# A gated cross-attention and router block on one core: the third piece of c gets another buffer and an earlier load, and the fillers of the last three pairs change places

## The chip, the core and the metric

The kernel runs on one core of a Trainium2 chip. The core has a matrix engine (TensorE, in the profile PE; its weight loads, which overlap with it, are PEld), a vector engine (VectorE, DVE), a scalar engine (ScalarE, ACT), a general engine (GpSimd, POOL) and a queue engine (SyncE, SP) that issues most of the transfers; ACT issues a few as well. Each engine runs its own instructions in the order in which they are written, and engines wait for each other through semaphores. The metric is the device time of one execution in microseconds, the median of several executions; lower is better.

## What is computed

The inputs are x and c, each 8 batches of 512 rows by 2048 columns in f32. Columns are cut into windows of 128. Cut to its core, the reference is

```python
n = layernorm(x, axis=-1)                      # over the 2048 columns of a row
q, k = Wq @ n + bq, Wk @ n + bk                # 256 rows each, per window
val = Wv @ c + bv
scores = q_h.T @ k_h / sqrt(32)                # 8 heads, 128 x 128 per window
o = gelu(softmax(masked(scores)) @ val_h)      # per head
x = x + tanh(g_xattn) * (Wo @ o + bo) * mask
flat = layernorm(x, axis=-1)                   # again over the 2048 columns
s = softmax(flat @ router_weight.T + router_bias)        # 64 experts
w = s with all but its 8 largest set to 0
x = x + tanh(g_ffn) * (flat * w.sum() + w @ expert_bias)
```

## The kernel before

**Tiling.** 512 columns make a chunk `ch` (0 to 31, four to a batch) and 256 columns, two windows, make a pair `g` (0 to 63), so that pair g is half `h = g % 2` of chunk `g // 2`. The 512 rows of x and c are four groups m of 128 partitions. `cx` tiles hold a half chunk of c (128 x 4 x 256, 512 KB), and two buffers of them rotate; `o` tiles (128 x 2 x 512, of the same size) hold the attention output of a chunk, also in two buffers.

**The start.** SP and ACT issue the loads of the weights, of x of batch 0 in 16 tiles of 256 KB (four groups m, four chunks j) and of the first c pieces (lines 153 to 174). PE first makes the values `pv = c.T Wv` of the pieces (0,0), (0,1) and (1,0) (`values`, L404, its products at L410), and then the first queries and keys (`first_queries_and_keys`, L332, products `pf` at L339), one group m after the other. Group m needs the normalised x of that group: DVE takes its statistics (L263, four of them, and L246), POOL turns them into a scale and a shift in a chain of small instructions (L248 to L276), ACT applies them (`norm`, L284). The piece (1,0) has to wait until PE has read the first buffer of `cx`.

**The loop.** Slots g = 0 to 61 (L789) each run the scores of pair g, the softmax (maxima on DVE at L454, exponentials on ACT at L463, division on POOL at L472), the transposes of pair g-1 (`turn` on PE at L486, its copy on ACT at L492), the weighing of pair g-2 (`weigh`, L505, copy L515), and fillers for PE: queries and keys of the next chunk (L373), its values (L410), the output projection (`attend`, L534), transposes of finished x (`turn_x`, L558), router logits (L572), the choice of experts (`select`, L632, on DVE; `turn_weights`, L655, two transposes `pw` on PE at L661, and a copy on ACT at L665) and the mix of the experts' biases (`mix`, L691, with the addition on DVE at L702). The order on every engine is that in which the lines stand; nothing is rescheduled. The choice of experts for the batch that ended before falls on every eighth slot, the last of these being slot 60.

Each slot has the values of the next chunk among its fillers, by

```python
vals = [] if (nxt, h) == (1, 0) or nxt == last else [(nxt, h)]    # L806
```

so that slots 60 and 61, whose next chunk is the last (31), have none. In slot 60 the part behind the queries and keys runs

```python
turn_x_(2)
for c_, h_ in vals:
    values(c_, h_, 0, 0)
    turn_(2)
    values(c_, h_, 1)
...
turn_weights(b4)
```

**The end.** Pairs 62 and 63 (`h0` and `g`, lines 998 to 1050) are written out by hand. `z` is chunk 31 and `b` is batch 7, so `turn_x(z - 2, k)` transposes columns of chunk 29 and `mix(b - 1, k)` finishes part k of batch 6. Values of (31,0) stand in pair 62, values of (31,1), two mixes and the four transposes of chunk 29 in pair 63. The transposes of attention, `turn_x` and the product of `weigh` share two PSUM buffers (tag `tr`); a buffer comes free when the copy out of it is done, which is ACT's for `turn` and `weigh`, and DVE's for these `turn_x`. Projections, values and mixes share two others (tag `mm`).

Of the kernel before, what the change touches and what calls it, by code (L numbers as in the profile page):

```python
# [9 lines left out]
F32 = mybir.dt.float32  # L10
# [6 lines left out]
P = 128  # L17
# [18 lines left out]
def flamingo_gated_kernel(  # L36
# [23 lines left out]
    nc = tc.nc  # L60
# [6 lines left out]
    NM = D // P  # L67
# [5 lines left out]
    HW = NPP * W  # L73
    NH = CW // HW
# [9 lines left out]
    work = ctx.enter_context(tc.tile_pool(name="work", bufs=2))  # L84
# [6 lines left out]
    def columns(ch):  # L91
        return slice((ch % NCH) * CW, (ch % NCH + 1) * CW)

    def rows_of(t, b, cs):
        return t[b, :, cs].rearrange("(m p) s -> p m s", p=P)
# [13 lines left out]
        nc.sync.dma_start(t, rows_of(x, ch // NCH, columns(ch)))  # L109
        xn[ch] = t  # L110

    def load_cx(ch, h, queue=nc.sync):
        t = work.tile([P, NM, HW], F32, tag="cx", name=f"cx_{ch}_{h}")
        s0 = (ch % NCH) * CW + h * HW
        queue.dma_start(t, rows_of(c, ch // NCH, slice(s0, s0 + HW)))
        cxs[ch, h] = t

    def load_mask(ch):
        t = work.tile([P, CW], F32, tag="mk", name=f"mk_{ch}", bufs=4)
        nc.sync.dma_start(t, masks[ch // NCH, :, columns(ch)].to_broadcast([P, CW]))  # L120
        mks[ch] = t

    def load_xr(ch, queue=nc.sync):

        t = work.tile([P, NM, CW], F32, tag="xr", name=f"xr_{ch}", bufs=6)
        queue.dma_start(t, rows_of(x, ch // NCH, columns(ch)))
        xr[ch] = t
# [20 lines left out]
    def load_first_x(m):  # L148
        for j in range(NCH):
            queue_ = nc.scalar if j >= NCH // 2 and m < NM - 1 else nc.sync  # L150
            queue_.dma_start(xr[j][:, m, :], x[0, m * P : (m + 1) * P, columns(j)])

    nc.sync.dma_start(wv_sb, wvT.rearrange("(m p) e -> p m e", p=P))
    load_cx(0, 0, nc.scalar)
    load_first_x(0)
    load_cx(0, 1)
    nc.sync.dma_start(wq_sb, wqT.rearrange("(m p) e -> p m e", p=P))
    nc.scalar.dma_start(wk_sb, wkT.rearrange("(m p) e -> p m e", p=P))
    load_first_x(1)

    def load_rest():
        load_cx(1, 0)
        load_first_x(2)
        load_first_x(3)
        load_mask(0)
        nc.sync.dma_start(bv_sb, bv.partition_broadcast(P))
        with nc.allow_non_contiguous_dma(reason="short bias vectors onto partitions"):
            nc.sync.dma_start(bq_sb, bq.rearrange("(t p) -> p t", p=P))
            nc.sync.dma_start(bk_sb, bk.rearrange("(t p) -> p t", p=P))
            nc.sync.dma_start(bo_sb, bo.rearrange("(t p) -> p t", p=P))  # L170
        nc.sync.dma_start(gates[:, 0:1], g_xattn.partition_broadcast(P))
        nc.sync.dma_start(gates[:, 1:2], g_ffn.partition_broadcast(P))
        nc.sync.dma_start(rb_sb, rb.partition_broadcast(P))
        load_mask(1)
# [148 lines left out]
    def product(shape, name, r=None):  # L323

        if late:
            late.append(late.pop(0))
            r = late[0]
        if r is not None:
            return ps_sc.tile(shape, F32, tag=f"sc{r}", name=name)
        return ps_mm.tile(shape, F32, tag="mm", name=name)  # L330
# [73 lines left out]
    def values(ch, h, i, r=None):  # L404

        if (ch, h) not in pvs:
            pvs[ch, h] = product([P, NPP, DK], f"pv_{ch}_{h}", r)
        cx, pv = cxs[ch, h], pvs[ch, h]
        for m in range(NM):
            nc.tensor.matmul(  # L410
                pv[:, i, :], cx[:, m, i * W : (i + 1) * W], wv_sb[:, m, :],
                start=(m == 0), stop=(m == NM - 1),
            )

    def values_out(ch, h):
        pv = pvs.pop((ch, h))
        del cxs[ch, h]
        vT = work.tile([P, NPP, DK], F32, tag="vT", name=f"vT_{ch}_{h}", bufs=4)
        nc.vector.tensor_tensor(vT, pv, bv_sb[:, None, :].to_broadcast([P, NPP, DK]), ALU.add)
        vTs[ch, h] = vT  # L420
# [35 lines left out]
    def exps(g, q):  # L456

        p = pairs[g]
        i = q // 2
        for r in (2 * (q % 2), 2 * (q % 2) + 1):  # L460
            for e in range(NE):
                h = e * HR + r
                nc.scalar.activation(  # L463
                    p["at"][i][:, h, :], p["sc"][r][:, i, e, :], AF.Exp,
                    bias=p["nmx"][:, r, i, e : e + 1], accum_out=p["rsum"][:, i, h : h + 1],
                )

    def divide(g, i, engine=None):
        p = pairs[g]
        rs = p["rsum"][:, i, :]  # L470
        nc.vector.reciprocal(rs, rs)  # L471
        (engine or nc.gpsimd).tensor_tensor(  # L472
            p["at"][i], p["at"][i], rs[:, :, None].to_broadcast([P, H, W]), ALU.mult
        )
# [3 lines left out]
    def turn(g, k):  # L478

        p = pairs[g]  # L480
        i, e = k // NE, k % NE
        if e == 0:
            p["atT"][i] = work.tile([P, H, W], F32, tag="atT", name=f"atT_{g}_{i}")
        pt = ps_tr.tile([P, HR, W], F32, tag="tr", name=f"pt_{g}_{k}")
        for r in range(HR):
            nc.tensor.transpose(pt[:, r, :], p["at"][i][:, e * HR + r, :], ident)  # L486
        p["pt"] = pt

    def turned(g, k):
        p = pairs[g]  # L490
        i, e = k // NE, k % NE
        nc.scalar.copy(p["atT"][i][:, e * HR : (e + 1) * HR, :], p.pop("pt"))  # L492
# [33 lines left out]
    def gelu(ch, cs=whole):  # L526
        o = os_[ch][:, :, cs]
        nc.scalar.activation(o, o, AF.Gelu)
# [26 lines left out]
    def turn_x(ch, k, engine=None):  # L555
        px = ps_tr.tile([P, NM, P], F32, tag="tr", name=f"px_{ch}_{k}")
        for m in range(NM):
            nc.tensor.transpose(px[:, m, :], xr[ch][:, m, k * P : (k + 1) * P], ident)  # L558
        t = work.tile([P, NM, P], F32, tag="x1T", name=f"x1T_{ch}_{k}", bufs=4)
        if engine is nc.vector:  # L560
            nc.vector.tensor_copy(t, px)
        else:
            nc.scalar.copy(t, px)  # L563
        x1T[ch, k] = t
# [117 lines left out]
    def mix(b, k, hold=False):  # L682

        t = experts[b]
        j, mp = k // 2, k % 2
        js = slice(j * CW, (j + 1) * CW)
        held[b, k] = []
        for i in range(2):
            rows = slice(i * E, (i + 1) * E)
            pt = product([P, CW], f"pb_{b}_{k}_{i}")  # L690
            nc.tensor.matmul(pt, t["wT"][rows, mp, :], eb_sb[rows, js], start=True, stop=True)  # L691
            held[b, k].append(pt)
        if not hold:
            added(b, k)

    def added(b, k, queues=(nc.sync,)):
        j, mp = k // 2, k % 2
        ch = b * NCH + j
        n = 2 // len(queues)
        for i, pt in enumerate(held.pop((b, k))):  # L700
            xc = xr[ch][:, 2 * mp + i, :]
            nc.vector.tensor_tensor(xc, pt, xc, ALU.add)  # L702
            if (i + 1) % n == 0:
                ms = slice(2 * mp + i + 1 - n, 2 * mp + i + 1)
                queues[i // n].dma_start(rows_of(out, b, columns(ch))[:, ms, :], xr[ch][:, ms, :])
        if mp == 1:
            del xr[ch]
# [26 lines left out]
    for i in range(NPP):  # L734
        values(0, 0, i)
    new_queries_and_keys(0)
    load_rest()

    nc.scalar.activation(spare, half[:, 0:1], AF.Identity)
# [29 lines left out]
    queue = [(b, i) for b in range(1, B) for i in range(NPIECE)]  # L769
# [17 lines left out]
    last = NC - 1  # L787
    pieces_left = [(b, i) for b in range(1, B) for i in range(NPIECE)]
    for g in range(NG - NH):  # L789
        ch, h = g // NH, g % NH  # L790
        even = h == 0
        nxt = ch + 1
# [10 lines left out]
        lch = ch - 2 if not even and ch >= 2 else None  # L803
        pch = ch - 1 if not even and ch >= 1 else None

        vals = [] if (nxt, h) == (1, 0) or nxt == last else [(nxt, h)]  # L806
        b4 = ch // NCH - 1
        fin = g % SPB if b4 >= 0 else None

        def turn_(k):  # L810
            if g1 is not None:
                turn(g1, k)
                turned(g1, k)
# [172 lines left out]
    z, b, h0 = last, B - 1, NG - NH  # L986
# [20 lines left out]
    divide(h0, 0)  # L1007
    turn_(h0 - 1, 0, 1)
    exps(h0, 2)
    values(z, 0, 0)  # L1010
    turn_(h0 - 1, 2)
    exps(h0, 3)
    values(z, 0, 1)
    values_out(z, 0)
    turn_(h0 - 1, 3)
    divide(h0, 1)

    scores(g)
    weigh(h0 - 1)
# [2 lines left out]
    maxima(g, (2, 3))  # L1022
    turn_(h0, 0)
    exps(g, 0)
    mix(b - 1, 2)
    turn_(h0, 1)
    exps(g, 1)
    divide(g, 0)
    values(z, 1, 0)
    turn_x(z - 2, 0, nc.vector)  # L1030
    exps(g, 2)
    values(z, 1, 1)
    values_out(z, 1)
    exps(g, 3)
    divide(g, 1)
    turn_(h0, 2)
    turn_x(z - 2, 1, nc.vector)
    turn_(h0, 3)
    turn_x(z - 2, 2, nc.vector)
    gelu(z - 1)  # L1040
    mix(b - 1, 3)
    load_xr(z)
    turn_x(z - 2, 3, nc.vector)
    weigh(h0)
    weighed(h0)
    for k in (4, 5):
# [110 lines left out]
```

## Time and profile before

| | us |
|---|---|
| median of 3 runs (1336.63 to 1337.97) | 1337.61 |
| the profiled execution | 1337.72 |
| its span, first to last instruction | 1335.9 |
| PE busy | 1306.5 |
| DVE, ACT, POOL busy | 887.2, 836.0, 793.1 |
| mean granted clock of PE, as a share of full speed | 0.995 |
| transfers, 173.32 MB in all | 130 GB/s on average |

The profiled execution is 0.11 us above the median, and its span leaves 1.8 us of it to what lies before the first and behind the last instruction. Times below are microseconds from the start of the span. A row of a timeline gives start, duration, engine, line, operation, the tiles, how often, and in brackets how long the engine had been idle before it and what ended that idle time. A row of waits gives the time in total, how often, and the longest. A row of a stretch gives its length, the busy time and count of each engine in it, PE's granted clock, the share of the DMA engines and GB/s. The page's "chain that ended last" is the path of work, followed back from the last instruction, that set the time.

### The profile page before, as it was taken

What the parts mean: (1) busy time and instruction counts of PE and PEld (TensorE: products, weight loads), DVE (VectorE), ACT (ScalarE), POOL (GpSimd) and SP (SyncE); (2) the same over time, 40 slices, a digit from 0 to 9 for tenths busy, and PEclk for the clock granted to TensorE, in tenths of its full rate; (3) what the DMA queues carried; (4) which work ended last, traced back from release to release, by engine and by line L of the source; (5) the groups of instructions that cost most, each with busy time, mean ns of one, the idle gap of its engine ahead of it and who ended that gap; (6) DMA issues with size and microseconds to landing.
All of it is one profiled execution on the core that took longest, in us unless ns stands there. A gap on an engine that the chain in (4) does not pass through costs nothing.

```text
span 1335.9 us, 26509 instructions
## 1 busy us (share of the span) xinstructions
PE 1306.5 (98%) x9802; PEld 953.6 (71%) x9802; DVE 887.2 (66%) x1815; ACT 836.0 (63%) x2843; POOL 793.1 (59%) x802
## 2 busy tenths in 40 slices
PE   7999999999999999999999999999999999999997
PEld 4677777777777777777777777777777777777653
DVE  5666666576766766677666676667676675666566
ACT  2567756666755666756667566667656767656653
POOL 3545556565566755667555667556566665566652
PEclk8999999999999999999999999999999999999999
DMA  9423332334443534443534443524544423332124
GB/s 290 117 73 124 98 103 99 131 105 133 150 163 115 166 102 136 150 146 131 166 100 138 151 148 130 166 89 135 165 146 132 156 65 120 135 112 87 64 80 173
DMA packets 109729, 173.32 MB, mean 130 GB/s; under 512 B 9248, under 2 KB 43680, under 8 KB 109472
## 3 DMA queue, kind: packets, MB, share of 16 engines
q1 hardware_dynamic: 107536, 168.75, 39.1%
q10 hardware_dynamic: 2064, 2.88, 0.6%
q8 instruction: 77, 1.26, 0.4%
q14 instruction: 52, 0.43, 0.1%
HBM read 138.06 MB, written 33.55 MB: 128 GB/s over the span
## 4 chain that ended last, share of the span: by engine, by line
PE 93%; DVE 3%; ACT 2%; DMA 1%; issue 0%; DVEq 0%; ACTq 0%
PE qk L373 27%; PE po L534 17%; PE pv L410 15%; PE pt L486 8%; PE pa L505 5%; PE pb L691 5%; PE pl L572 4%; PE sc L442 4%; PE px L558 4%; PE sc L433 2%; ACT at L463 1%; PE pf L339 1%; DMA cx<-in_ctx 1%; DVE st L553 1%; DVE st L263 1%; PE pg L602 1%
## 5 line engine op out<-in xcount | busy, mean ns | idle before, releaser
L472 POOL TENSOR_TENSOR at<-at,rsum 128x1024 f32<-128x1024 f32 x128 | 244.3, 1908 | 282.2 <-DVE rsum L471 259.6
L463 ACT ACTIVATE at<-sc,nmx 128x128 f32<-128x128 f32 x1024 | 364.9, 415 | 5.8 <-DVE nmx L454 5.8
L463 ACT ACTIVATION_READ_ACCUMULATOR at<-sc,nmx 128x1 f32 x1024 | 261.4, 255 | 0.0
L410 PE MATMUL pv<-wv_sb,cx 128*128 128x256 f32 x1024 | 242.7, 386 | 9.8 <-DMA cx<-in_ctx 9.6
L534 PE MATMUL po<-o,wo_sb 128*128 128x512 f32 x512 | 234.0, 599 | 0.0
L410 PEld LDWEIGHTS pv<-wv_sb,cx 128*128 128x128 f32 x1024 | 191.4, 194 | 33.8 <-DMA cx<-in_ctx 10.0
L543 POOL TENSOR_TENSOR xr<-t,xr 128x512 f32<-128x512 f32 x124 | 160.4, 1294 | 88.7 <-DVE t L540 88.2
L515 ACT COPY o<-pa 128x512 f32<-128x512 f32 x64 | 37.5, 585 | 258.2 <-PE pa L505 258.2
L492 ACT COPY atT<-pt 128x512 f32<-128x512 f32 x256 | 151.4, 622 | 56.2 <-PE pt L486 55.7
L454 DVE TENSOR_REDUCE nmx<-sc 128x4 f32<-128x512 f32 x256 | 158.7, 682 | 12.0 <-PE sc L442 12.0
L534 PEld LDWEIGHTS po<-o,wo_sb 128*128 128x128 f32 x512 | 94.2, 190 | 100.1 <-issue 92.8
L540 DVE SCALAR_TENSOR_TENSOR t<-po,bo_sb,mk 128x512 f32<-128x512 f32 x128 | 95.9, 750 | 100.6 <-PE po L534 99.9
L486 PEld LDWEIGHTS pt<-ident,at 128*128 128x128 f32 x1024 | 122.0, 141 | 56.9 <-issue 36.4
L486 PE MATMUL pt<-ident,at 128*128 128x128 f32 x1024 | 150.8, 275 | 1.3 <-ACT atT L492 1.1
L563 ACT COPY x1T<-px 128x512 f32<-128x512 f32 x120 | 70.3, 585 | 118.8 <-PE px L558 117.1
L373 PE MATMUL qk<-xt,wq_sb 128*128 128x256 f32 x496 | 128.2, 381 | 1.3 <-DVE u L381 1.3
L373 PE MATMUL qk<-xn,wk_sb 128*128 128x256 f32 x496 | 127.6, 380 | 0.0
L373 PE MATMUL qk<-xn,ws 128*128 128x256 f32 x496 | 127.3, 379 | 0.0
L373 PEld LDWEIGHTS qk<-xn,ws 128*128 128x128 f32 x496 | 94.2, 190 | 12.8
L702 DVE TENSOR_TENSOR xr<-pb,xr 128x512 f32<-128x512 f32 x124 | 79.2, 684 | 33.0 <-PE pb L691 33.0
L373 PEld LDWEIGHTS qk<-xn,wk_sb 128*128 128x128 f32 x496 | 89.3, 190 | 10.0 <-DVE lgT L588 0.3
L678 POOL TENSOR_SCALAR xr<-xr,xa,xd 128x512 f32<-128x512 f32 x120 | 94.4, 797 | 0.8
(119 smaller groups left out, 2008.4 us busy)
## 6 DMA issues: line engine op xcount, KB each, us to landing
cx<-in_ctx SPq DMA_DIRECT2D x63, 512.0 KB, 5.4
out_dram<-xr SPq DMA_DIRECT2D x60, 512.0 KB, 3.5
raw<-in_x SPq DMA_DIRECT2D x112, 256.0 KB, 3.5
xn<-in_x SPq DMA_DIRECT2D x28, 1024.0 KB, 7.5
xr<-in_x SPq DMA_DIRECT2D x28, 1024.0 KB, 7.8
mk<-in_mask_Bx1x_ff SPq DMA_DIRECT2D x32, 256.0 KB, 5.4
xr<-in_x SPq DMA_DIRECT2D x10, 256.0 KB, 5.9
out_dram<-xr SPq DMA_DIRECT2D x7, 256.0 KB, 2.3
```

Source lines behind the costliest of these rows:

```text
L373: nc.tensor.matmul(out_, w_[:, j, es], xb[:, j, :], start=(j == 0), stop=(j == NM // 2 - 1))
L410: nc.tensor.matmul(pv[:, i, :], cx[:, m, i * W : (i + 1) * W], wv_sb[:, m, :], start=(m == 0), stop=(m == NM - 1),)
L454: nc.vector.tensor_reduce(p["nmx"][:, r, :, :], p["sc"][r], AX.X, ALU.max, negate=True)
L463: nc.scalar.activation(p["at"][i][:, h, :], p["sc"][r][:, i, e, :], AF.Exp, bias=p["nmx"][:, r, i, e : e + 1], accum_out=p["rsum"][:, i, h ...
L472: (engine or nc.gpsimd).tensor_tensor(p["at"][i], p["at"][i], rs[:, :, None].to_broadcast([P, H, W]), ALU.mult)
L486: nc.tensor.transpose(pt[:, r, :], p["at"][i][:, e * HR + r, :], ident)
L492: nc.scalar.copy(p["atT"][i][:, e * HR : (e + 1) * HR, :], p.pop("pt"))
L534: nc.tensor.matmul(po[:, cs], wo_sb[:, e, m * P : (m + 1) * P], os_[ch][:, e, cs], start=(e == 0), stop=(e == NE - 1),)
L540: nc.vector.scalar_tensor_tensor(t[:, cs], po[:, cs], bo_sb[:, m : m + 1], mks[ch][:, cs], ALU.add, ALU.mult)
L543: (engine or nc.gpsimd).tensor_tensor(xc, t[:, cs], xc, ALU.add)
L678: nc.gpsimd.tensor_scalar(xc, xc, a, d, ALU.mult, ALU.add)
L702: nc.vector.tensor_tensor(xc, pt, xc, ALU.add)
```

## The change

Three things change. `load_cx` takes a tag, and the piece (1,0) of c is loaded into a buffer of the tag `o`, with its load issued ahead of Wq and of the second group of x. The values of (31,0) move from pair 62 to slot 60. The fillers of pairs 62 and 63 are dealt anew: the second mix, two transposes of chunk 29 and the first half of the values of (31,1) move from pair 63 to pair 62; the fourth mix and the load of x for chunk 31 stand earlier in pair 63.

```diff
-    def load_cx(ch, h, queue=nc.sync):
-        t = work.tile([P, NM, HW], F32, tag="cx", name=f"cx_{ch}_{h}")
+    def load_cx(ch, h, queue=nc.sync, tag="cx"):
+        t = work.tile([P, NM, HW], F32, tag=tag, name=f"cx_{ch}_{h}")
...
     load_cx(0, 1)
+
+    load_cx(1, 0, tag="o")
     nc.sync.dma_start(wq_sb, wqT.rearrange("(m p) e -> p m e", p=P))
     nc.scalar.dma_start(wk_sb, wkT.rearrange("(m p) e -> p m e", p=P))
     load_first_x(1)
 
     def load_rest():
-        load_cx(1, 0)
         load_first_x(2)
...
-        vals = [] if (nxt, h) == (1, 0) or nxt == last else [(nxt, h)]
+        vals = [] if (nxt, h) in ((1, 0), (last, NH - 1)) else [(nxt, h)]
...
     divide(h0, 0)
     turn_(h0 - 1, 0, 1)
     exps(h0, 2)
-    values(z, 0, 0)
+    mix(b - 1, 2)
     turn_(h0 - 1, 2)
     exps(h0, 3)
-    values(z, 0, 1)
-    values_out(z, 0)
     turn_(h0 - 1, 3)
+    turn_x(z - 2, 0, nc.vector)
+    turn_x(z - 2, 1, nc.vector)
     divide(h0, 1)
+    values(z, 1, 0)
 
     scores(g)
...
     turn_(h0, 0)
     exps(g, 0)
-    mix(b - 1, 2)
+    values(z, 1, 1)
+    values_out(z, 1)
     turn_(h0, 1)
     exps(g, 1)
     divide(g, 0)
-    values(z, 1, 0)
-    turn_x(z - 2, 0, nc.vector)
+    turn_x(z - 2, 2, nc.vector)
     exps(g, 2)
-    values(z, 1, 1)
-    values_out(z, 1)
+    mix(b - 1, 3)
+    load_xr(z)
     exps(g, 3)
     divide(g, 1)
     turn_(h0, 2)
-    turn_x(z - 2, 1, nc.vector)
+    turn_x(z - 2, 3, nc.vector)
     turn_(h0, 3)
-    turn_x(z - 2, 2, nc.vector)
     gelu(z - 1)
-    mix(b - 1, 3)
-    load_xr(z)
-    turn_x(z - 2, 3, nc.vector)
     weigh(h0)
```

## The prediction

> **What bounds the kernel now.** First the busy shares and the chain of waits.
>
> ```profile
> PE 1306.5 (98%) x9802; PEld 953.6 (71%) x9802; DVE 887.2 (66%) x1815; ACT 836.0 (63%) x2843; POOL 793.1 (59%) x802
> PE 93%; DVE 3%; ACT 2%; DMA 1%; issue 0%; DVEq 0%; ACTq 0%
> ```
>
> PE is the bound. The change gives PE no less to do, so it can only gain from time in which PE stands still or runs slowly. That is 1335.9 - 1306.5 = 29.4 us of idleness, of which 6.5 lie before the first product and 7.5 behind the last. PE's own waits name the rest that is large:
>
> ```profile
> PE pv L410 <- DMA cx<-in_ctx: 9.6, 2, 6.5
> PE pw L661 <- DVE rest L648: 3.0, 1, 3.0
> ```
>
> The 9.6 are the first wait of 6.5 and one of 3.1. PE's timeline shows where these two idle times lie, and what follows them: the start (four rows), then slot 60 (three rows).
>
> ```profile
> 6.48 9.91 PE L410 MATMUL pv<-wv_sb,cx 128*128 128x256 f32 x32 [6.48 <-DMA cx<-in_ctx]
> 19.48 6.78 PE L410 MATMUL pv<-wv_sb,cx 128*128 128x256 f32 x16 [3.09 <-DMA cx<-in_ctx]
> 26.10 1.88 PE L339 MATMUL pf<-xn,wq_sb 128*128 128x512 f32 x4
> 36.40 1.88 PE L339 MATMUL pf<-xn,wq_sb 128*128 128x512 f32 x4
> ```
> ```profile
> 1232.99 0.60 PE L486 MATMUL pt<-ident,at 128*128 128x128 f32 x4
> 1236.55 0.44 PE L661 MATMUL pw<-ident,rest 128*128 128x128 f32 x2 [2.95 <-DVE rest L648]
> 1238.06 2.08 PE L691 MATMUL pb<-eb_sb,wT 64*128 64x512 f32 x4
> ```
>
> After each, PE is slow: 16 products of values take 6.62 us (19.48 to 26.10), and four mixes 2.08, where they take 1.13 elsewhere. The stretches show why; the number behind POOL's is the granted clock.
>
> ```profile
> 19.40:21.00 1.60, 1.52 (x4) 1.25 (x5) 0.86 (x2) 0.00 (x0) 1.27 (x6) 0.50 1.06 389
> 1233.00:1235.00 2.00, 0.59 (x6) 0.35 (x4) 1.93 (x9) 1.07 (x2) 0.96 (x1) 1.00 0.00 0
> 1238.50:1239.50 1.00, 1.00 (x4) 0.07 (x2) 0.00 (x0) 0.25 (x1) 1.00 (x2) 0.50 0.00 0
> ```
>
> The clock is halved from about 18.9 to 25.6 and from 1237.4 to 1240.9, after the idle time.
>
> **Part 1, the third piece of c.** The load of (1,0) waits until PE has read the first buffer, is issued at 12.97 and lands at 19.44. Changed, it waits for no reader. In the changed program's order it takes the place that Wq's load had on SP, behind the landing of c's piece (0,0): issue at 6.45. Wq in that place landed 8.8 us later (row of its transfer), so the piece lands at about 15.3, before PE ends with (0,1) at 16.39. The 3.09 us go, and with them the halved clock: warm, 16 products take 3.46 (the values of other slots stand in the chain of waits with 3.46). PE is ready for `pf` at 16.39 + 3.46 = 19.85 instead of 26.10, **6.25 earlier**.
>
> Next late is x. In the trace `pf` needs 3.43 per group (26.10, 29.54, 32.97, 36.40) and x is there in time: normalised x of group 1 starts at 21.32, of group 3 at 29.23, each tile 0.8. But SP's queue now carries 512 KB more ahead of group 1, and SP waits longer: x of group 1 was issued at 7.70 behind the landing of an x tile, and is now issued behind (0,1) and Wk, at 12.2 to 12.5. The stretches from 3.2 to 23 run at 355 to 389 GB/s with DMA share above 1, so no reordering makes the whole faster: what had landed by 19.44 (all but six x tiles) is what will have landed when group 1 is complete, so its last tile comes at 18 to 19.4; I take 19.2. From there by the durations of the trace: three more statistics to 21.1; then 2.84 from there to ACT (18.48 to 21.32) and 0.8, so group 1 at 24.75 against PE's 19.85 + 3.43 = 23.28: a wait of 1.45. DVE does group 2 to 24.0 and group 3 to 26.8 (2.56 plus 0.27 each); group 3 needs 3.91 more (25.32 to 29.23) and 0.8: 31.5, against PE's 24.75 + 2 x 3.43 = 31.6. So the last `pf` group starts at 31.6 instead of 36.40: **4.8**. Ends: x at 18.0 leaves 6.1; x another 1.5 us later leaves 3.3. I round the middle to **5.0**. Everything behind (sums of x on POOL, first softmax) hangs on the same chain and moves along. The second buffer rotation costs nothing: (1,1) is needed 30 us after its load, and `o` is first written in slot 2.
>
> **Part 2, slot 60.** The values of (31,0), 3.46, now stand between `pt` and `pw`. Slot 52, where they always stood, shows PE without a wait:
>
> ```profile
> 1074.39 1.89 PE L410 MATMUL pv<-wv_sb,cx 128*128 128x256 f32 x8
> 1076.12 0.38 PE L661 MATMUL pw<-ident,rest 128*128 128x128 f32 x2
> ```
>
> PE reaches `pw` at 1232.99 + 0.43 + 3.46 = 1236.9, DVE's `rest` is there at 1236.5. The wait of 2.95 and the slow clock go. Warm, `pw`, two transposes and the mix take 0.22 + 0.44 + 0.53 + 1.06 = 2.2, so pair 61 begins at 1239.1, and its weighing at 1240.3 instead of 1241.65: **1.35 earlier**, though 3.46 of work came in. The DVE addition of 0.69 for these values follows `select` and delays nothing that PE waits for.
>
> **Part 3, pairs 62 and 63.** Here 3.46 has gone, yet ACT paces the pair. Its copies in the trace:
>
> ```profile
> 1266.11 0.59 ACT L492 COPY atT<-pt 128x512 f32<-128x512 f32 x1
> 1268.22 0.58 ACT L492 COPY atT<-pt 128x512 f32<-128x512 f32 x1
> 1277.60 0.63 ACT L492 COPY atT<-pt 128x512 f32<-128x512 f32 x1
> 1278.98 0.58 ACT L492 COPY atT<-pt 128x512 f32<-128x512 f32 x1 [0.75 <-PE pt L486]
> ```
>
> With the scores of pair 62 left where they were (1257.05), PE now does mix (1.06 from 1263.68) and two transposes, and is through at 1265.65. The next transpose needs the buffer of the third `pt`, whose copy stands on ACT behind four exponentials that end at 1266.0: 1266.5. The one after it needs DVE's copy (0.69): 1267.85. Then 0.43 and 1.73 of values: scores of pair 63 at 1270.0 instead of 1268.11. Pair 63 has lost 3.66 of PE work, but the fourth `pt` waits for the third's copy, which stands behind all eight exponential groups: 10.35 after the scores; its own copy ends at 11.55, and `weigh` ends at 11.9 where it ended at 13.86 (1268.11 to 1281.97). Sum: 12.95 + 11.9 = 24.85 against 11.06 + 13.86 = 24.92. The 3.46 us less work is eaten by new waits; only slot 60's 1.35 remains. At the next meeting point (`pt`, then `attend` of chunk 30 at 1284.77) PE waits about 0.3 for ACT's copy behind GELU. I count **1.2** for parts 2 and 3. The earlier load of x (31) shortens nothing: it landed 2 us before its use. The mix's addition, moved ahead, costs DVE 1.3 in a pair where it is busy for 5.63 of 11.1.
>
> **A rule against it.** PE waits in pair 63 from 6.85 to 8.05 and 8.5 to 10.35 after the scores, with one transpose (0.43) between. The row of slot 60 says that a hole of 2.95 followed by transposes halves the clock for 3.4 us, at a cost of about 1.7. [...] By the row alone (a window with 0.9 of 3.4 busy was enough) the window must fall well: about 3 in 10. [...] Sum by the one 5.0 + 1.2, by the other 5.0 - 0.3. No trace shows a hole filled with one transpose; I lean to the row and keep both ends.
>
> **Cases.** The sum is made against the profiled 1337.72, 0.11 above the median.
> - *Both parts as worked out*, 0.48: 1337.7 - 6.2 = **1331.5**, own range 1330.3 to 1332.5.
> - *Clock halved in pair 62 or 63*, 0.28: 1.5 back, 1333.0 (1332.5 to 1334.5). [...]
> - *x comes later or in worse order*, 0.11: the start gains 2.5, the rest 0.6: 1334.6. For it: the moved issues at 12.2; against: saturated transfers.
> - *ACT is no pace* (copies earlier than I place them, holes filled), 0.08: slot 60's 2.95 + 1.7 and 0.6 of small waits come out whole: 1337.7 - 5.0 - 5.2 = 1327.5. Against: ACT's rows stand back to back from 1263.5 to 1268.7.
> - *Piece (1,0) still late*, so that only the end changes, 0.02: 1336.5.
> - *Slower*, 0.03: SP's loads form a chain, each behind the landing of an earlier one, and with one more large load ahead the last x tiles slip. They land at about 23.5 now; PE has 6.4 in hand on group 3 as it stands. From a landing about 6 + 2.7 later, at 32, PE is later than before by more than can be told apart: 1341. The saturated stretches speak against it.
>
> Range 1329.3 to 1334.8. What a measurement can tell from no change is about 0.2%, 2.7 us, so 1334.9 and below is faster: 0.48 + 0.27 + 0.07 + 0.08 = 0.90; within 0.2% 0.07; slower 0.03.
>
> **What would show it.** `pv` of (1,0) starts without a wait at 16.4 with clock 1.00; a wait of 1 to 2 us before the second `pf` group; scores of pair 0 at about 35 instead of 39.9; `pw` of slot 60 without a wait; new PE waits on ACT's L492 and DVE's copies of about 1.7 us in pair 62 and 3 in pair 63. Wrong if `pf` starts at 19.9 but its last group not before 34, if the clock is 0.50 behind pair 63, or if pairs 62 and 63 run without these waits.

## The result, and the profile after

| | before | after |
|---|---|---|
| median, us | 1337.26 | 1334.11 |
| lowest to highest of 16 runs each | 1333.41 to 1338.19 | 1332.85 to 1335.98 |
| the profiled execution | 1337.72 | 1334.19 |
| its span | 1335.9 | 1332.4 |

The changed kernel is faster: ratio 0.9978, 95% interval 0.9971 to 0.9986. It moved by 3.15 us (3.53 between the two profiled executions), about half of the 6.2 that were forecast. The page after, busy shares and the chain that ended last:

```profile
PE 1303.9 (98%) x9802; PEld 951.6 (71%) x9802; DVE 887.1 (67%) x1815; ACT 837.1 (63%) x2843; POOL 794.3 (60%) x802
PE 92%; DVE 3%; DMA 2%; ACT 1%; issue 1%; POOL 0%; SPq 0%; DVEq 0%; ACTq 0%
```

PE still runs 9802 instructions, and its busy time fell by 2.6 us: a slow clock shows as busy time (the four mixes of slot 60 are 2.08 of it before and 1.13 after), so time won at the clock shows here. PE's waits (total, times, longest):

```profile
PE pv L411 <- DMA cx<-in_ctx: 6.8, 1, 6.8
PE pt L487 <- ACT atT L493: 2.6, 2, 1.8
...
PE px L559 <- DVE x1T L562: 1.6, 2, 0.8
PE pf L340 <- ACT xn L285: 1.4, 1, 1.4
```

The second wait for c (3.1) and the one of `pw` (3.0) are gone. In their place stand the three last rows, of which the prediction had named all: normalised x at `pf`, ACT's copy of a `pt`, DVE's copy of a `px`. Of the 2.6 behind ACT's copies only the 1.8 are new; a wait of 0.8 early in the loop was there before. The start in PE's timeline:

```profile
6.75 13.52 PE L411 MATMUL pv<-wv_sb,cx 128*128 128x256 f32 x48 [6.75 <-DMA cx<-in_ctx]
20.11 1.88 PE L340 MATMUL pf<-xn,wq_sb 128*128 128x512 f32 x4
...
25.11 1.98 PE L340 MATMUL pf<-xn,wq_sb 128*128 128x512 f32 x4 [1.41 <-ACT xn L285]
...
32.08 1.88 PE L340 MATMUL pf<-xn,wq_sb 128*128 128x512 f32 x4
```

All 48 products of values stand in one row without a hole. The one wait behind them is 1.41, and the last `pf` group starts at 32.08 instead of 36.40. Slot 60:

```profile
1231.05 1.89 PE L411 MATMUL pv<-wv_sb,cx 128*128 128x256 f32 x8
1232.78 0.38 PE L662 MATMUL pw<-ident,rest 128*128 128x128 f32 x2
...
1233.96 1.13 PE L692 MATMUL pb<-eb_sb,wT 64*128 64x512 f32 x4
...
1236.24 1.08 PE L506 MATMUL pa<-atT,vT 128*32 128x128 f32 x32
```

`pw` no longer waits, and the four mixes take 1.13 instead of 2.08: the granted clock is 1.00 from 1233.9 to 1235.1, where before it was 0.50 from 1237.9 to 1240.1. The last row is the weighing in slot 61, which before started at 1241.65:

```profile
1241.65 1.08 PE L505 MATMUL pa<-atT,vT 128*32 128x128 f32 x32
```

Now the place where time was lost, pairs 62 and 63:

```profile
1261.17 0.63 PE L559 MATMUL px<-ident,xr 128*128 128x128 f32 x4 [0.60 <-issue]
1262.58 0.66 PE L559 MATMUL px<-ident,xr 128*128 128x128 f32 x4 [0.78 <-DVE x1T L562]
...
1264.90 0.40 PE L434 MATMUL sc<-mneg,negw 32*128 32x512 bf16 x4
...
1272.83 0.66 PE L559 MATMUL px<-ident,xr 128*128 128x128 f32 x4 [0.81 <-DVE x1T L562]
1275.30 0.89 PE L487 MATMUL pt<-ident,at 128*128 128x128 f32 x4 [1.81 <-ACT atT L493]
1276.12 1.94 PE L506 MATMUL pa<-atT,vT 128*32 128x128 f32 x32
1277.99 2.41 PE L573 MATMUL pl<-x1T,rw_sb 128*64 128x512 f32 x8
```

The two holes of pair 63 (0.81 and 1.81) are there with one group of transposes between them, and behind them PE is slow: the weighing takes 1.94, where it takes 1.08 in slot 61. The stretches of the hole and of what follows it (busy time of each engine; the number behind POOL's is the granted clock):

```profile
1272.15:1275.57 3.42, 0.92 (x6) 0.69 (x7) 2.59 (x6) 3.10 (x17) 2.29 (x2) 1.00 0.19 75
1275.57:1279.00 3.43, 3.43 (x40) 2.01 (x40) 0.00 (x1) 2.74 (x3) 3.43 (x4) 0.50 0.50 135
```

PE was busy for 0.92 of 3.42 us, 27%, and the granted clock was then 0.50 for a stretch as long.

### The profile page after: what moved, and what is told of

Its sections match the earlier page's. It is cut to its first block, busy times and chain, and to the rows that moved or that the text cites. A ratio compares the mean times of both kernels' runs of the same rounds, so it can differ in the third digit from the quotient of the medians.

```text
span 1332.4 us, 26505 instructions
## 1 busy us (share of the span) xinstructions
PE 1303.9 (98%) x9802; PEld 951.6 (71%) x9802; DVE 887.1 (67%) x1815; ACT 837.1 (63%) x2843; POOL 794.3 (60%) x802
## 4 chain that ended last, share of the span: by engine, by line
PE 92%; DVE 3%; DMA 2%; ACT 1%; issue 1%; POOL 0%; SPq 0%; DVEq 0%; ACTq 0%
PE qk L374 27%; PE po L535 17%; PE pv L411 15%; PE pt L487 8%; PE pa L506 5%; PE pb L692 5%; PE pl L573 4%; PE sc L443 4%; PE px L559 4%; PE sc L434 2%; ACT at L464 1%; PE pf L340 1%; DVE st L264 1%; DMA cx<-in_ctx 1%; DVE st L554 1%; PE pg L603 1%
## 5 line engine op out<-in xcount | busy, mean ns | idle before, releaser
L411 PE MATMUL pv<-wv_sb,cx 128*128 128x256 f32 x1024 | 239.4, 383 | 6.8 <-DMA cx<-in_ctx 6.8
```

The source lines that it names most:

```text
L411: nc.tensor.matmul(pv[:, i, :], cx[:, m, i * W : (i + 1) * W], wv_sb[:, m, :], start=(m == 0), stop=(m == NM - 1),)
```

## The experiments

Each is compared with the kernel before on the same chip; (n) is the number of runs. Every edit starts from the changed kernel.

### The start alone

The buffer and the earlier load stay; slot 60 and pairs 62 and 63 go back to what they were.

```diff
-        vals = [] if (nxt, h) in ((1, 0), (last, NH - 1)) else [(nxt, h)]
+        vals = [] if (nxt, h) == (1, 0) or nxt == last else [(nxt, h)]
...
```

(The fillers of pairs 62 and 63, as they stood before, are left out here.)

> The start of the change alone (c's third piece early, in a buffer of o), slots 60 to 63 as before. Theory: the start is worth 4.1 us (the scores of pair 60 came 4.1 earlier in the changed trace), x of group 1 is its limit, and slot 60 keeps its wait of 2.95 and its halved clock: 1333.2, as fast as the whole change or faster. Rival, that the two parts share one gain (what the start saves is lost again in a later wait, and the end brings the rest): 1335 or more.

Median 1333.34 (9), against 1336.42 (21): ratio 0.9977, interval 0.9967 to 0.9986. That is as much as the full change gains (0.9978). In its PE timeline slot 60 is as it was, only 4.5 us earlier (`pw` stood at 1236.55):

```profile
1232.06 0.44 PE L662 MATMUL pw<-ident,rest 128*128 128x128 f32 x2 [2.96 <-DVE rest L649]
...
1233.71 2.08 PE L692 MATMUL pb<-eb_sb,wT 64*128 64x512 f32 x4
```

The wait of 2.96 and the slow mixes stand, and pair 63 has no halved clock (1.00 from 1270 to 1280, and its weighing takes 1.08). So what the other two parts win in slot 60 (the change's own trace shows it) is lost again elsewhere.

### The end alone

```diff
-    load_cx(1, 0, tag="o")
...
     def load_rest():
+        load_cx(1, 0)
         load_first_x(2)
```

> The end of the change alone, the start as before. Theory: slot 60 gives 1.3, pairs 62 and 63 take 1.9 back through copies that wait behind ACT's exponentials and a halved clock: 1337.8, within 0.6 of before, and where the clock is not halved behind pair 63, 1336.6. Rival, that the end gains (values in slot 60 are worth their 4.6 us of wait and slow clock): 1333 to 1335.

Median 1336.72 (13), against 1336.42: ratio 0.9999, interval 0.9990 to 1.0007. Slot 60's values and the new deal of pairs 62 and 63 together are worth nothing that can be measured; a gain of more than 1.3 us (0.0010 of 1336.4) lies outside the interval. Its profiled execution had the full clock in pair 63 (1.00 from 1275 to 1280, the weighing 1.17), and there the last row of mixes starts at 1319.21, where before it started at 1319.90: 0.7 us.

### Group 1 of x ahead of Wq

The timeline of SP's queue after the change shows what the new load pushed back: x of group 1 is issued at 12.22 (before: 7.70).

```profile
2.22 4.89 SPq L115 DMA_DIRECT2D cx<-in_ctx  x2
7.66 0.37 SPq L159 DMA_DIRECT2D wq_sb<-in_L_xattn_Wq  x1
12.22 7.70 SPq L151 DMA_DIRECT2D xr<-in_x  x8
```

```diff
     load_cx(1, 0, tag="o")
+    load_first_x(1)
     nc.sync.dma_start(wq_sb, wqT.rearrange("(m p) e -> p m e", p=P))
     nc.scalar.dma_start(wk_sb, wkT.rearrange("(m p) e -> p m e", p=P))
-    load_first_x(1)
```

> The whole change, with the second group of x issued ahead of Wq and Wk. Theory: x of group 1 is what PE waits for (1.41) at the start; with 512 KB less ahead of it on SP it is complete 1.2 us earlier, Wq lands last but in time for 20.1, the wait shrinks to 0.2 and all groups move by about 1.2: 1332.9. Rival, that transfers are saturated and one wait only takes the place of the other (Wq or Wk late): no better than 1334.1, the wait under Wq's or Wk's name.

Median 1332.23 (5), against 1336.42: ratio 0.9963, interval 0.9950 to 0.9977. DVE's timeline, after the change first, then this kernel:

```profile
18.86 2.54 DVE L264 BATCH_NORM_STATS2 st<-xr 128x6 f32<-128x512 f32 x4 [7.66 <-DMA xr<-in_x]
```
```profile
15.81 2.56 DVE L264 BATCH_NORM_STATS2 st<-xr 128x6 f32<-128x512 f32 x4 [4.72 <-DMA xr<-in_x]
```

Group 1's statistics start 3.05 earlier, and PE's wait for x is gone: in this kernel's PE timeline no `pf` shows a wait, and the last group starts at 29.98 instead of 32.08.

```profile
19.45 1.96 PE L340 MATMUL pf<-xn,wq_sb 128*128 128x512 f32 x4
...
22.96 1.88 PE L340 MATMUL pf<-xn,wq_sb 128*128 128x512 f32 x4
...
26.40 1.88 PE L340 MATMUL pf<-xn,wq_sb 128*128 128x512 f32 x4
...
29.98 1.98 PE L340 MATMUL pf<-xn,wq_sb 128*128 128x512 f32 x4
```

So after the change x of group 1 is what the start waits for, and the order of the loads sets it. The first product came earlier in this profile too (6.08, not 6.75), but that is not the reason: in the run with DVE copies below it came at 6.20, with Wq ahead of x, and the last `pf` group still started at 31.89.

### Copies of the last `pt` on DVE

The third and fourth copies of `turn` in each of pairs 62 and 63 go from ACT, where they stand behind the exponentials, to DVE, and in pair 63 the two transposes are written ahead of the last exponentials.

```diff
-    def turned(g, k):
+    def turned(g, k, copy=None):
...
-        nc.scalar.copy(p["atT"][i][:, e * HR : (e + 1) * HR, :], p.pop("pt"))
+        (copy or nc.scalar.copy)(p["atT"][i][:, e * HR : (e + 1) * HR, :], p.pop("pt"))
...
-    turn_(h0 - 1, 2)
+    turn(h0 - 1, 2)
+    turned(h0 - 1, 2, nc.vector.tensor_copy)
...
-    turn_(h0 - 1, 3)
+    turn(h0 - 1, 3)
+    turned(h0 - 1, 3, nc.vector.tensor_copy)
...
-    divide(g, 0)
     turn_x(z - 2, 2, nc.vector)
-    exps(g, 2)
     mix(b - 1, 3)
     load_xr(z)
+    turn(h0, 2)
+    turned(h0, 2, nc.vector.tensor_copy)
+    divide(g, 0)
+    turn_x(z - 2, 3, nc.vector)
+    turn(h0, 3)
+    turned(h0, 3, nc.vector.tensor_copy)
+    exps(g, 2)
     exps(g, 3)
     divide(g, 1)
-    turn_(h0, 2)
-    turn_x(z - 2, 3, nc.vector)
-    turn_(h0, 3)
```

> The whole change, but the copies of the third and fourth transposes of pairs 61 and 62 are made by DVE, and in pair 63 these transposes stand before the last exponentials. Theory: ACT's queue paces pairs 62 and 63; weigh of pair 62 then ends about 10.1 us after the scores of pair 63 instead of 13.1, no hole over 1 us is left before it, the clock stays full: 1331.0. Rival, that the clock alone is to blame: the scores of pair 63 stay 2.2 us later than before and the gain is 1.2, to 1332.9. Rival, that DVE becomes the pace (its copies queue behind maxima and additions): no gain, 1334.

Median 1330.48 (5, all between 1330.38 and 1330.54), against 1336.42: ratio 0.9953, interval 0.9941 to 0.9966. PE's timeline of pair 63:

```profile
1264.25 0.40 PE L434 MATMUL sc<-mneg,negw 32*128 32x512 bf16 x4
...
1272.84 0.66 PE L487 MATMUL pt<-ident,at 128*128 128x128 f32 x4 [1.02 <-DVE atT L493]
1273.51 1.20 PE L506 MATMUL pa<-atT,vT 128*32 128x128 f32 x32
1274.64 1.94 PE L573 MATMUL pl<-x1T,rw_sb 128*64 128x512 f32 x8
```

From the scores to the logits (`pl`) behind `weigh` are 10.4 us (13.1 after the change, 12.1 in its repetition below, where the clock was full), the hole is 1.02, and the weighing takes 1.20 with a granted clock of 1.00 from 1272 to 1276. ACT's order was the pace of pair 63, and it was ACT that held PE in the hole. Two gains are mixed in the median. All five runs had a mean granted clock of 0.998 or 0.999; against the runs of the changed kernel with such a clock (1332.85 to 1333.19) this kernel is 2.4 us faster, and the rest comes from the clock. In pair 63 the copies and the order of the transposes changed together, and what each of the two gives was not measured.

### Both

The edits of the last two experiments together.

```diff
     load_cx(1, 0, tag="o")
+    load_first_x(1)
...
+    turned(h0 - 1, 2, nc.vector.tensor_copy)
```

> The second group of x ahead of Wq and Wk, and the four copies on DVE, together. Theory: the start's limit and the end's limit are independent, so their gains over the change (1.9 and 3.6 us by the medians of those runs) add up: 1328.7. Rival, that both draw on the same slack: no better than 1330.5.

Median 1328.78 (5, 1328.59 to 1328.87), against 1336.57 (34): ratio 0.9940, interval 0.9928 to 0.9953. This beats both kernels. The two repairs add up: over the change they brought 0.0015 and 0.0025 of the time alone, and bring 0.0038 together.

### Pairs 62 and 63 not filled again

The start and slot 60's values as changed; pairs 62 and 63 as before, only without the values of (31,0).

```diff
     exps(h0, 2)
-    mix(b - 1, 2)
     turn_(h0 - 1, 2)
     exps(h0, 3)
     turn_(h0 - 1, 3)
-    turn_x(z - 2, 0, nc.vector)
-    turn_x(z - 2, 1, nc.vector)
     divide(h0, 1)
-    values(z, 1, 0)
...
```

> The start and the values of (31,0) in slot 60 as in the change, but nothing moved into their place: pairs 62 and 63 keep the order of before without these values. Theory: ACT paces the pairs, so the refill brings nothing: scores of pair 63 come 10.9 us after those of pair 62 (13.25 with the refill, 11.06 before), pair 63 is as long as before (13.9 to the end of weigh), and the whole is 1332.1 with a full clock and 1333.8 where the hole of 2.7 in pair 62 halves it, so between 0 and 1 us faster than the change. Rival, that the refill is worth what it moves (PE paces the pairs): 2 to 3 us slower than the change, 1336 to 1337.

Median 1333.88 (15), against 1336.57: ratio 0.9977, interval 0.9969 to 0.9985. This is the theory's case with the halved clock; three runs, at 1331.90 to 1332.02 with a mean clock of 0.998, are taken for its case with the full one. The hole has only moved. With nothing in the slot, PE waits for ACT's exponentials at the scores of pair 63 and the clock falls there; PE's timeline, then the stretch ahead of the fall and one behind it:

```profile
1260.55 0.37 PE L434 MATMUL sc<-mneg,negw 32*128 32x512 bf16 x1 [0.33 <-ACT at L464]
1261.73 1.28 PE L434 MATMUL sc<-mneg,negw 32*128 32x512 bf16 x2 [0.81 <-ACT at L464]
```
```profile
1258.25:1261.66 3.41, 1.92 (x12) 1.12 (x11) 0.14 (x2) 3.41 (x16) 3.13 (x2) 1.00 0.78 298
...
1264.00:1266.00 2.00, 2.00 (x41) 1.68 (x39) 1.45 (x3) 0.00 (x0) 0.65 (x1) 0.50 0.00 0
```

Here the clock fell with PE busy for 1.92 of 3.41 us, 56%, and no hole over 0.81. By the medians, filling pair 62 with work from pair 63 is worth nothing, because PE was not what pair 62 waited for. With the full clock it costs 1.0 us (1332.9 against 1331.9).

### 14 products in the hole

Products whose result is overwritten are put ahead of the last transposes of chunk 29, to keep PE busy in the hole.

```diff
-    def turn_x(ch, k, engine=None):
+    def turn_x(ch, k, engine=None, extra=0):
...
+        for r in range(extra):
+            nc.tensor.matmul(px[:, r % NM, :], ident, xr[ch][:, r % NM, k * P : (k + 1) * P], start=True, stop=True)
...
-    turn_x(z - 2, 3, nc.vector)
+    turn_x(z - 2, 3, nc.vector, extra=14)
```

> The whole change with 14 extra products of 128x128 by 128x128, whose output the last transpose of chunk 29 overwrites, put in front of that transpose: 1.5 us of work in the hole of 1.81 in pair 63, where PE waits for ACT's copy. Theory: the extra work costs nothing, since it lies in the wait, and it keeps the clock from being halved: every run near 1332.9, where the change had 1332.9 in 4 of 16 runs and 1334.1 or more in the others. Rival, that the three groups of times have another cause: the same spread as the change, median 1334.1. Rival, that PE paces the pair: 1.5 us slower.

Median 1334.26 (17), against 1336.57: a miss. The timeline shows that the filling was too long:

```profile
1272.88 3.39 PE L559 MATMUL px<-xr,ident 128*128 128x128 f32 x28 [0.80 <-DVE x1T L564]
1276.11 0.60 PE L561 MATMUL px<-ident,xr 128*128 128x128 f32 x4
1276.55 0.60 PE L487 MATMUL pt<-ident,at 128*128 128x128 f32 x4
1277.49 1.08 PE L506 MATMUL pa<-atT,vT 128*32 128x128 f32 x32 [0.35 <-DVE x1T L564]
```

The 14 products are 28 instructions of 0.12 us, so that the last `pt` starts 1.25 us later than in the changed kernel. The clock stayed full (1.00 from 1276.5 to 1278.5, where the weighing takes 1.08; the mean clock of all 17 runs is 0.997 to 0.999), and the delay gave back what that won.

### 14 transposes in the hole

In the loop of the run before, a transpose takes the place of the product.

```diff
+            nc.tensor.transpose(px[:, r % NM, :], xr[ch][:, r % NM, k * P : (k + 1) * P], ident)
```

> As the run before, but the 14 extra operations are transposes. If transposes do not count as activity, the clock is halved as in the change: median 1334.1. If they count as products do, it is the time of the run with products, 1332.9. The wait itself is the same in both.

Median 1332.88 (8, seven of them between 1332.64 and 1333.04), against 1336.57: ratio 0.9971, interval 0.9961 to 0.9981.

```profile
1272.88 1.75 PE L559 MATMUL px<-ident,xr 128*128 128x128 f32 x14 [0.80 <-DVE x1T L564]
1274.46 0.60 PE L561 MATMUL px<-ident,xr 128*128 128x128 f32 x4
1275.34 0.66 PE L487 MATMUL pt<-ident,at 128*128 128x128 f32 x4 [0.28 <-ACT atT L493]
1275.93 1.17 PE L506 MATMUL pa<-atT,vT 128*32 128x128 f32 x32
```

The same hole, filled with transposes alone: the last `pt` starts when it did in the changed kernel (1275.34, 1275.30), and the weighing takes 1.17 instead of 1.94. In seven of the eight runs (mean clock 0.998 or 0.999) transposes held the clock; the eighth took 1334.46 with a mean clock of 0.997.

### 7 products in the hole

The run with 14 products, with half as many.

```diff
-    turn_x(z - 2, 3, nc.vector)
+    turn_x(z - 2, 3, nc.vector, extra=7)
```

> As the run with 14 extra products, but with 7: an f32 product of 128x128 showed as two passes, so that 14 took 3.2 us and overran the wait; 7 take 1.6, as 14 transposes do. Theory: they lie in the wait and hold the clock: 1332.9 in most runs, as with the transposes. Rival, that plain products hold the clock less well than transposes or cost time of their own: 1334.

Median 1332.82 (6, 1332.71 to 1333.28), against 1336.64 (13): ratio 0.9967, interval 0.9955 to 0.9980. The mean clock of all six is 0.998 or 0.999. Without the overrun, products do what transposes do.

### The changed kernel once more

No edit; beside the last experiment on the same chip.

> The changed kernel once more, beside the run before on the same chip: 1334.1 in most runs, with some at 1332.9 (clock full behind pair 63) and some at 1336 (halved twice). If it gives 1332.9 in most runs here, the extra operations are not what held the clock.

Median 1334.21 (8), against 1336.64: ratio 0.9977, interval 0.9967 to 0.9988. Two runs took 1332.98 and 1333.19, six 1334.12 to 1334.61. Its profiled execution was one of the two, and its PE timeline has the same hole without the slow clock:

```profile
1275.37 0.65 PE L487 MATMUL pt<-ident,at 128*128 128x128 f32 x4 [1.81 <-ACT atT L493]
1275.95 1.17 PE L506 MATMUL pa<-atT,vT 128*32 128x128 f32 x32
```

So one and the same program, with the same hole of 1.81, has the clock halved in some executions and not in others. Beside it, on the same chip, the 7 products kept the clock in six runs of six, so the extra operations are what held it.

## Why the prediction was right, and where it was not

**The direction and the mechanism held.** Each wait that was to go went, and each that was to come came at the named instruction. The time lies inside the range, 2.6 us above the forecast and 0.7 below the upper end. The start and the clock make up most of the 2.6. The range held because it also took in the case that was thought less likely, the halved clock; the central sum did not hold.

**The start was forecast at 5.0 and gave 4.1.** At the scores of pair 60 the changed kernel is 4.12 ahead (1214.88 against 1219.00). The steps were good: x of group 1 issued at 12.2 (measured 12.22), a wait of 1.45 before the second `pf` group (1.41). But the last `pf` group came at 32.08, not 31.6: the statistics of group 1 were done at 21.40, not at 21.1, and small steps behind them took 0.2 more. The sum of 4.8 was rounded up to 5.0, and 0.2 of the 4.3 were lost between `pf` and pair 60. The mechanism was right, and the term was 0.9 too large. That x of group 1 is the limit is shown by the third experiment.

**Slot 60 was forecast at 1.35 and gave 1.29**: the weighing in slot 61 starts 5.41 earlier (1236.24 against 1241.65), of which 4.12 are the start's.

**Pairs 62 and 63 were rightly called ACT's.** From the scores of pair 62 to those of pair 63 are 13.25 us (forecast 12.95). The last `pt` comes 10.40 behind the scores of pair 63 (forecast 10.35). From these scores to the logits behind `weigh` are 13.09 with the slow clock, and 12.10 in the repetition without it (forecast 11.9). The new waits were 1.38 in pair 62 and 2.62 in pair 63 (forecast about 1.7 and 3); the first 0.60 of them, which the profile puts down to "issue", ended 0.10 behind an ACT copy (1260.45 + 0.62). The repetition is 4.05 ahead at the scores of pair 60 and 4.73 at the projection of chunk 30 (1280.04 against 1284.77), so with the full clock parts 2 and 3 give 0.7 of the forecast 1.2, as the end alone did in its profile (1319.90 to 1319.21). In the change's own profile, with the clock halved, that projection starts at 1281.26, 3.51 ahead: parts 2 and 3 cost 0.6 there. So of the 6.2 forecast, 4.1 - 0.6 = 3.5 were left: 0.9 too much in the start, 0.5 in small terms of the end, 1.3 in the clock.

That ACT paces was then shown: two copies taken off ACT in each pair bring the ratio from 0.9978 to 0.9953, some 3.3 us, of which about 2.4 remain when runs with the full clock are compared. Filling pair 62 or leaving it makes no difference to the ratio (0.9978, 0.9977). This disposes of the case "ACT is no pace". "Piece (1,0) still late" falls by the one row of 48 products. Of "x comes later" and "slower" the mechanism is real, since the order of SP's loads costs 2 us (0.9978 against 0.9963), but that is already within the wait of 1.41 and its late statistics, and it never came near the size that either needed.

**The clock was the wrong case.** "Clock halved in pair 62 or 63" got 0.28 and 1.5 us, "both parts as worked out" 0.48. The changed kernel's 24 runs fall into six at 1332.85 to 1333.19, sixteen at 1333.98 to 1334.61, and two at 1335.95 and 1335.98; the mean granted clock is 0.998 or 0.999 in the six and 0.996 or 0.997 in all others. The profiled execution of the first kind has the full clock behind pair 63, that of the second kind the halved one. So the halved clock was the likeliest outcome, in 18 of 24 runs if the two highest are counted with it, and its price is 1.2 us. The prediction had itself named "the clock is 0.50 behind pair 63" as a sign of being wrong, and it came. The failing step was "the window must fall well: about 3 in 10", the author's estimate, which no run shows; the runs give 18 of 24 in its place. The row of slot 60 said that a window with 0.9 of 3.4 busy was enough; pair 63 has just such a window (0.92 of 3.42), so the row itself spoke for the halving. It said that 0.9 was enough, not that more would be too much: after the change the clock also fell at 1326.78, at the end, behind a stretch with PE busy for 1.49 of 3.41. The hole of slot 60 lies in one piece, with transposes in front and behind; that this one had a group of transposes in the middle was taken for a protection. In three executions of four it was none.

Of the two sums, 5.0 - 0.3 was nearer to the 3.5 that came. Its -0.3, the 1.2 of parts 2 and 3 less an estimated 1.5 for the halved clock, came as -0.6 in the profile after, and as 0.7 in the repetition with the full clock. Transposes held the clock as products did: 14 transposes in the hole kept it in seven of eight runs and 7 products in six of six, against six of 24 with the hole. The one group of four that stands between the two holes was too little. The longest hole here was 1.81, against 2.95 in slot 60.

**Why only in some executions.** In the traces the falls of the granted clock lie whole steps of 3.41 us apart, the length of the halved stretch of pair 63 (1275.58 to 1278.99). Before, it fell at 18.89 and at 1237.45: 1218.56 us, or 357 steps of 3.4133. After, it fell at 1275.58 and at 1326.78, 15 such steps apart; without the refill at 1261.66 and 1329.93, 20 steps. Where this grid lies against the program differs between two profiles of the same program: after the change a border lies at 1272.17, in the repetition at 1273.80. In the profile after, one step of it (1272.17 to 1275.58, within 0.02 us the stretch shown above) covers nearly all of both holes. In the repetition, whose clock next fell at 1328.42, 16 steps behind 1273.80, a border of the grid lies in the longer hole:

```profile
1270.39:1273.80 3.41, 2.36 (x13) 1.13 (x12) 1.72 (x4) 3.41 (x20) 1.35 (x1) 1.00 0.00 0
1273.80:1277.21 3.41, 1.84 (x38) 1.32 (x40) 1.01 (x3) 2.65 (x9) 2.51 (x3) 1.00 0.42 156
```

Two steps share the idle time, each has PE busy for more than half (69% and 54%), and the clock stays full. Cut in this way, the profiles before and after show from 13 us on, as long as PE still has work, a full clock that fell behind the steps with PE busy for 26% and 27% (before) and for 27% and 44% (after), and stayed full behind all with 59% or more. Between these lie the 54% of the repetition, behind which it stayed, and the 56% of the run without the refill, behind which it fell. So PE's busy time alone gives no sharp border here. If one is put at half, an estimate from the 44% and the 54%, a step that starts anywhere from 1271.04 to 1273.67 of the repetition lowers the clock, 2.6 of 3.41 us or 77% of the possible positions. This too is an estimate, from its PE rows; 18 of 24 runs are 75%. No run moved the grid on purpose, so this rests on the profiles as they fell.

**The base.** The profile against which the sum was made, 1337.72, stands in the upper part of the runs of before, whose medians on other chips were 1336.42 to 1336.64. Most of those runs too lie in two groups about 1.2 apart (1336.0 to 1336.9, 1337.1 to 1338.2). A sum from one execution carries this spread.

## What to carry to other kernels

Ask which engine sets the pace of a stretch before filling it: work moved between pairs 62 and 63 changed nothing in the median, and moving the copies that free PE's buffers off ACT's queue, with the transposes written earlier, gave some 3.3 us, 2.4 of them without the clock. When a load is put ahead, look at what it pushes back on the same queue: with the load that was needed next kept ahead of a less urgent one, the same edit gave another 2 us. Here PE's busy time in steps of 3.41 us told more about the clock than the longest hole did: two holes of 0.81 and 1.81 with 0.66 of transposes between them were enough, and even work without use kept the clock, and won time where it ended before the hole would have (1332.8 and 1332.9 with 7 products or 14 transposes, 1334.3 with 14 products). The same hole lowered the clock in 18 of 24 executions of one program and not in the other six, so a single profile does not tell whether a hole costs the clock.

## What was not expected of the hardware

- The clock fell with no hole longer than 1.81 us, behind a stretch in which PE was 27% busy, and only in 18 of 24 executions of the same program; without the refill it fell behind a stretch in which PE was 56% busy, with no hole over 0.81.
- A product of two f32 tiles of 128 x 128 shows as two instructions (14 gave 28, 3.39 us), a transpose of the same size as one (14 in 1.75 us).
- One stretch of 3.4 us at half clock costs about 1.2 us, not 1.7: by the rows of the changed kernel and its repetition `pt`, the weighing and the logits lose 0.24 + 0.77 + 0.47, and the transposes behind win back 0.2 (1.09 and 1.28), so that the projection is 1.22 later (1.29 counted from the last `pt`).
